# Layer 3 of a four-layer network from sums of the token-major residual, with layer 0's output statistics on ACT and the gate's factor on POOL

## The chip, the cores and the metric

The program runs on one core of a Trainium2 chip. A core has a matrix engine (TensorE; PE in the profile, with its weight loads as PEld), a vector engine (VectorE, DVE), an activation engine (ScalarE, ACT), a general engine (GpSimd, POOL) and a sequencer that mostly issues transfers (SyncE, SP). They run side by side, each through its own queue in order, and wait for one another on semaphores. SBUF and PSUM are the on-chip memories; the products of PE go to PSUM. The metric is the device time of one execution in microseconds; the profile is one further execution with its trace.

## The reference

Input is `x` of 16 images of 64 x 64 tokens with 256 channels, in f32. Each of four layers adds its output on the group-normalised input to that input:

```python
x = x + L0(gn(x), embeddings)   # nearest of 1024 codes by distance, its row is returned
x = x + L1(gn(x), Wf, bf, Wg, bg, Wh, bh)   # sigmoid attention inside each row of 64 tokens
x = x + L2(gn(x), w1, b1, w2, b2, w3, b3)   # a gate per token, from a softmax over 4096 x 4096
x = x + L3(gn(x), w_qkv, w_out, b_out, gamma, beta)   # linear attention, then a layer norm
```

`gn` has 32 groups of 8 channels over all tokens. The part that the change rewrites most is layer 3:

```python
q, k, v = split(x @ w_qkv)            # 4 heads of 32
q = softmax(q, over the 32 of a head) * 32 ** -0.5
k = softmax(k, over all tokens)
context = einsum('bhdn,bhen->bhde', k, v)
out = einsum('bhde,bhdn->bhen', context, q)      # back to tokens
out = out @ w_out + b_out
out = (out - mean) * rsqrt(var + 1e-3) * gamma + beta   # over the channels
```

## The kernel before

An image (a batch in what follows) has 4096 tokens. Work goes in 8 chunks of 512 tokens (`CH` = 4 tiles of 128), channel-major as two tiles of 128 channels (`NK` = 2). Between layers the activations pass through DRAM, one 512 KB tile for each chunk.

Every layer is a Python generator that emits instructions and yields a number now and then. At the end of the kernel each layer of each batch gets a start and a length in units of the code search, and a heap interleaves the generators by these, so that in the middle of the run the search of one batch lies beside layer 1 of the one before, the exponentials of another and layer 3 of a fourth. The yields set how much of one generator goes between two pieces of another. The framework puts what is emitted into the engines' queues by priority and by its own estimate of readiness; on the chip each queue then runs in order.

The pieces that matter here:

- `stage1` is layer 0. For each tile of 128 tokens PE computes products with 1024 codes (L377), ACT makes the row `nn` of squared lengths (L372), DVE adds and takes the maximum (L384) and finds its place (L389), and POOL gathers the code's row and adds it to the token-major input by an indirect DMA (L390). `back` turns a finished chunk back to channel-major by PE transposes (L352), ACT copies it out of PSUM (L355), and DVE takes statistics of it (`chunk_stats`, L249, aggregated at L256 in `gn_finish`).
- `layer1` has its projections at L457 and L468, `rows2` the three rows of layer 2, `stage2` the 4096 x 4096 exponentials: L617 on ACT and L620 on DVE, 1024 of each, 2048 elements wide.
- `gate2` loads the gates spread over the partitions (`gb`, one buffer), ACT forms the factor `u` = 1 + scale * gate (L674), DVE multiplies (L675) and takes statistics.
- `stage3` is layer 3 in two passes over the chunks. In the first, PE forms keys (L737) and, token-major, queries with values (L759, with a bias row at L763); ACT copies them (L764); keys get a running maximum and exponentials (L740 to L749); queries a softmax over each head by DVE and POOL (L778, L779, L780, and `normalize`, L726 to L728); the context is summed (L784, L786). The queries are transposed (L716) and stored. In between, the context becomes `wctx`, and a Gram matrix `gram` for the variance. In the second pass `form` multiplies the Gram matrix with the queries (L826, L828), `variance` sums this over partitions by matrix products with a column of ones (L834), ACT adds epsilon (L836), POOL takes the power -0.5 (L837), both one chunk ahead of use; PE forms the output (L854), ACT scales it (L857), PE transposes the residual (L859) and adds `x_row` (L863), DVE adds both (L865), and SP stores it.

PSUM has a pool `ps_m` of four banks that nearly all stages share through `bank`. `xb`, with three buffers, holds the chunks of the first statistics, of `rows2` and of both passes of layer 3.

Of the kernel before, what the change touches and what calls it, by code (L numbers as in the profile page):

```python
# [21 lines left out]
CH = 4  # L22
# [19 lines left out]
def kernel(  # L42
# [64 lines left out]
    nc.vector.memset(eps3, 1e-3)  # L107
# [17 lines left out]
    def row_tile(name):  # L125
        t = const.tile([P, C], BF16, name=name)
        nc.gpsimd.memset(t, 0.0)
        return t

    h_row, qv_row, x_row = row_tile("h_row"), row_tile("qv_row"), row_tile("x_row")  # L130

    def twice(row):
        return row.unsqueeze(1).to_broadcast([P, 2, C])

    def put_row(dst, v, weight, tag, plus=None):

        v3 = small.tile([P, NK, PARTS], F32, tag="v3", name=f"v3_{tag}")
        nc.scalar.copy(v3, v.unsqueeze(2).to_broadcast([P, NK, PARTS]))
        pb = bank(f"prow_{tag}")
        row = pb[:PARTS, :C]  # L140
        weight(row, v3, plus)

        for n in range(PARTS - 1):
            top = small.tile([PARTS, C], BF16, tag="ptop", name=f"top_{tag}_{n}", bufs=1)
            nc.scalar.copy(top, row)
            nc.tensor.matmul(row, lhsT=below[:, n, :], rhs=top, start=False, stop=True, skip_group_check=True)
        nc.scalar.copy(dst[0:PARTS, :], row)
# [47 lines left out]

    def centred(src, name):
# [22 lines left out]
    one = const.tile([P, 1], F32, name="one")  # L219
    nc.vector.memset(one, 1.0)  # L220
# [30 lines left out]
    def gn_finish(st, kind, b):  # L251

        tag = f"{kind}_{b}"
        mv = small.tile([P, NK, 2], F32, tag="gn_mv", name=f"mv_{tag}")
        for k in range(NK):
            nc.vector.bn_aggr(mv[:, k, :], st[:, k, :, :].rearrange("p c s -> p (c s)"))  # L256
        mean = mv[:, :, 0]
# [45 lines left out]
    def stage1(b):  # L303
        tag = f"s1_{b}"
        scale, _, nbias = norm0.pop(b)
# [39 lines left out]
        st1 = stats_tile(1, f"st1_{tag}")  # L345
        x1_d[b] = []

        def back(ch):
            for k in range(NK):
# [5 lines left out]
                nc.scalar.copy(xt[ch][:, k, :], pt)  # L355
            chunk_stats(st1, xt[ch], ch)
# [52 lines left out]
        with tc.high_priority(offset=URGENT):  # L409
            norm1[b] = gn_finish(st1, "n1", b)  # L410
# [5 lines left out]
    def layer1(b):  # L416
# [34 lines left out]
        def attend(ch):  # L451
# [14 lines left out]
            for t in range(CH):  # L466
# [5 lines left out]
                if t % 2 == 1:  # L472
                    nc.tensor.matmul(
                        ph[:, t - 1 : t + 1, :], lhsT=ones3, rhs=twice(h_row), start=False, stop=True, skip_group_check=True
# [178 lines left out]
    def gate2(b):  # L653
# [9 lines left out]
        for ch in range(NCHUNK):  # L663
# [8 lines left out]
            for k in range(NK):  # L672
                u = s3p.tile([P, CW], F32, tag="u2", name=f"u_{tag}_{ch}_{k}")
                nc.scalar.activation(u, gb, AF.Identity, bias=one, scale=scale[:, k : k + 1])  # L674
# [14 lines left out]
    def stage3(b):  # L689
# [6 lines left out]
        wqv_n = wts.tile([P, NK, 2 * P], F32, tag="wqv_n", name=f"wqv_{tag}")  # L696
        nc.sync.dma_start(out=wqv_n[:, :, 0:P], in_=w_src[:, :, 0, :])
        nc.sync.dma_start(out=wqv_n[:, :, P:], in_=w_src[:, :, 2, :])
        with tc.high_priority(offset=URGENT):
            scaled(wk_n, scale, nc.scalar)  # L700
            scaled(wqv_n, scale, nc.vector)
            put_row(qv_row, nmean, by_weight(wqv_n), f"qv_{tag}")
# [6 lines left out]
        ctxa = wts.tile([P, P], F32, tag="ctxa", name=f"ctx_{tag}")  # L709
        qvs, qTs = {}, []  # L710

        def queries(ch):
            qv = qvs.pop(ch)
            pq = bank(f"pq_{tag}_{ch}")
            for t in range(CH):
                nc.tensor.transpose(pq[:, t * P : (t + 1) * P], qv[:, t, 0, :], ident)  # L716
            qT = s3p.tile([P, CW], F32, tag="v2", name=f"qT_{tag}_{ch}", bufs=4)
            nc.scalar.activation(qT, pq, AF.Copy, scale=float(DH ** -0.5))
            qd_ = dram.tile([P, CW], F32, tag=f"qT_{ch}", name=f"qd_{tag}_{ch}")
            nc.scalar.dma_start(out=qd_, in_=qT)  # L720
            qTs.append(qd_)

        def normalize(ch):
            q4 = qvs[ch][:, :, 0, :].rearrange("p t (h d) -> p t h d", d=DH)
            qd = small.tile([P, CH, HEADS], F32, tag="qd", name=f"qd_{tag}_{ch}")
            nc.vector.tensor_reduce(qd, q4, AX.X, ALU.add)  # L726
            nc.vector.reciprocal(qd, qd)  # L727
            nc.gpsimd.tensor_tensor(q4, q4, qd.unsqueeze(3).to_broadcast([P, CH, HEADS, DH]), ALU.mult)  # L728

        for ch in range(NCHUNK):  # L730
# [14 lines left out]
            kx = s3p.tile([P, CW], F32, tag="v2", name=f"kx_{tag}_{ch}", bufs=4)  # L745
# [6 lines left out]
            qv = s3p.tile([P, CH, 2, P], F32, tag="u4", name=f"qv_{tag}_{ch}")  # L752
            qvs[ch] = qv
            for pr in range(CH // 2):
                pqv = bank(f"pqv_{tag}_{ch}_{pr}").rearrange("p (j n) -> p j n", j=2)
                for j in range(2):
                    t = 2 * pr + j
                    for k in range(NK):
                        nc.tensor.matmul(  # L759
                            pqv[:, j, :], lhsT=xt[:, k, t * P : (t + 1) * P], rhs=wqv_n[:, k, :],  # L760
                            start=(j == 0 and k == 0), stop=False, skip_group_check=True,
                        )
                nc.tensor.matmul(pqv, lhsT=ones3, rhs=twice(qv_row), start=False, stop=True, skip_group_check=True)  # L763
                nc.scalar.copy(qv[:, 2 * pr : 2 * pr + 2, :, :].rearrange("p j s n -> p j (s n)"), pqv)  # L764
            if ch == 0:
                put_row(x_row, xm_, by_identity, f"x_{tag}")
            yield 5
# [3 lines left out]
            ek = s3p.tile([P, CH, P], F32, tag="v2", name=f"ek_{tag}_{ch}", bufs=4)  # L771
            nc.scalar.copy(ek.rearrange("p t d -> p (t d)"), pkt)
            if ch > 0:
                queries(ch - 1)
# [170 lines left out]
```

## Time and profile before

| | |
|---|---|
| runs of the kernel | median 5933.36 us of 3 (5928.48 to 5943.17) |
| profiled execution | 5928.44 us, span 5926.7 us, mean clock of PE 0.941 |
| instructions | 79,561 |
| HBM | 751.18 MB read, 303.04 MB written, 178 GB/s over the span |
| L620 (DVE), L617 (ACT) | 1024 each; mean 2302 ns and 2088 ns |
| L377 (PE) | 4096 passes, mean 623 ns |
| L390 (POOL) | 512 gathers, mean 2067 ns |
| L779, L728 (POOL) | 128 each; mean 1818 ns and 1561 ns |

A busy time is the part of the span in which at least one instruction of the engine ran. For PE it includes the time in which a product drains, so the mean of a matmul is longer than what it keeps from the next one; an f32 matmul shows as two passes. In rows of waits the columns are the time in total, how often, and the longest. Every engine is busy nearly all of the run; the first 800 us or so fill the interleaving (layer 3 first appears at 807 us) and the last 130 us hold layer 3 of the last batch alone.

### The profile page before, as it was taken

The numbers are of one execution on the slowest core, as the hardware profiler recorded it, in microseconds if no ns is written. First come the engines' busy times: TensorE is split into PE (matmuls) and PEld (weight loads), VectorE is DVE, ScalarE is ACT, GpSimd is POOL, SyncE is SP. The second block draws the span as 40 slices with busy tenths as digits, with TensorE's granted clock in tenths as the row PEclk, the third lists the DMA queues.
The fourth block names the chain that finished last, engine by engine and source line by source line (L and its number), as shares of the span: only waits on it lengthen the run. The fifth ranks groups of instructions, "written<-read, shape, count | busy, mean of one in ns | idle before, by whom it ended". The sixth has DMA issues, their size and how long they took to land.

```text
span 5926.7 us, 79561 instructions
## 1 busy us (share of the span) xinstructions
PE 5337.4 (90%) x28239; PEld 3211.1 (54%) x28239; DVE 5121.1 (86%) x7282; ACT 4570.8 (77%) x6754; POOL 1939.4 (33%) x1314
## 2 busy tenths in 40 slices
PE   8968899889999999998989999898999989997777
PEld 3524465545656565564656556565555646564555
DVE  6499798989989898898989889898998989888882
ACT  4377687878778787887879788797878878787873
POOL 3122233224233332433334233342424333231331
PEclk9989999989999898999999899999999999998899
DMA  6544745555656656565665656656565664644543
GB/s 186 162 124 124 225 137 177 184 184 162 207 168 192 197 151 202 184 207 181 184 205 167 194 183 188 206 174 204 164 210 164 202 204 147 209 158 173 184 158 116
DMA packets 521380, 1059.47 MB, mean 179 GB/s; under 512 B 52504, under 2 KB 266392, under 8 KB 512792
## 3 DMA queue, kind: packets, MB, share of 16 engines
q1 hardware_dynamic: 406288, 885.11, 44.7%
q0 software_dynamic: 73728, 67.14, 7.9%
q10 hardware_dynamic: 40968, 102.13, 4.5%
q8 instruction: 224, 3.67, 0.3%
q14 instruction: 172, 1.41, 0.1%
HBM read 751.18 MB, written 303.04 MB: 178 GB/s over the span
## 4 chain that ended last, share of the span: by engine, by line
PE 48%; DVE 16%; ACT 12%; DMA 7%; issue 6%; POOL 4%; ACTq 0%; SPq 0%; POOLq 0%; DVEq 0%
PE pd_s L377 15%; DVE ex_s L620 6%; ACT ex_s L617 5%; PE ph_l L468 5%; PE pqv_s L759 3%; PE po_s L854 3%; PE pk_s L737 3%; PE po_l L506 2%; PE pr_r L565 2%; DMA xr_r<-x_l 2%; DVE i_s L389 2%; POOL qv_s L779 2%; PE pvr_s L834 1%; PE pz_s L826 1%; DMA qo_s<-qd_s 1%
## 5 line engine op out<-in xcount | busy, mean ns | idle before, releaser
L620 DVE CUSTOM_DVE_ANT_0 ex_s<-ex_s,x2b 128x2048 f32<-128x2048 f32 x1024 | 2350.7, 2302 | 46.2 <-ACT ex_s L617 44.9
L617 ACT ACTIVATE ex_s<-x0b,nmax_s,x_r 128x2048 f32<-128x2048 f32 x1024 | 2137.8, 2088 | 66.4 <-DVE num_s L620 60.3
L377 PE MATMUL pd_s<-e,xn_s 128*128 128x512 f32 x4096 | 2022.2, 623 | 43.5 <-DVE m L384 40.8
L390 POOL DMA_INDIRECT xc_s<-in_emb_rows,i_s x512 | 1058.1, 2067 | 2063.9 <-DVE i_s L389 1466.8
L377 PEld LDWEIGHTS pd_s<-e,xn_s 128*128 128x128 f32 x4096 | 754.4, 197 | 764.9 <-issue 669.1
L384 DVE CUSTOM_DVE_ANT_0 nd_s<-pd_s,nn_s 128x1024 f32<-128x1024 f32 x512 | 622.2, 1215 | 174.4 <-ACT nn_s L372 82.1
L389 DVE FIND_INDEX8 i_s<-m,nd_s 128x8 uint32<-128x1024 f32 x512 | 624.1, 1219 | 0.0
L372 ACT ACTIVATE nn_s<-ne,nx_s 128x1024 f32<-128x1024 f32 x512 | 583.2, 1141 | 21.5 <-DVE nx_s L343 15.7
L468 PE MATMUL ph_l<-wh_l,xt_l 128*128 128x256 f32 x2048 | 525.5, 393 | 28.3 <-DVE m L384 16.5
L759 PE MATMUL pqv_s<-wqv_s,xk_s 128*128 128x256 f32 x2048 | 494.6, 382 | 0.0
L759 PEld LDWEIGHTS pqv_s<-wqv_s,xk_s 128*128 128x128 f32 x2048 | 390.9, 192 | 127.5 <-issue 65.5
L468 PEld LDWEIGHTS ph_l<-wh_l,xt_l 128*128 128x128 f32 x2048 | 380.9, 193 | 143.8 <-issue 57.5
L837 POOL TENSOR_TENSOR lrs_s<-lrs_s,mhalf 128x4 f32<-128x4 f32 x128 | 183.0, 1429 | 749.3 <-ACT lrs_s L836 710.5
L857 ACT ACTIVATE y_s<-po_s,lrs_s 128x256 f32<-128x256 f32 x512 | 237.1, 469 | 214.8 <-PE po_s L854 166.2
L854 PE MATMUL po_s<-wctx_s,qo_s 128*128 128x256 f32 x1024 | 336.0, 415 | 32.3 <-ACT y_s L857 31.1
L506 PE MATMUL po_l<-at_l,h_l 64*128 64x64 f32 x4096 | 318.5, 297 | 46.2 <-DVE xt_l L511 42.7
L506 PEld LDWEIGHTS po_l<-at_l,h_l 64*128 64x128 f32 x4096 | 286.5, 206 | 108.5 <-DVE xt_l L511 48.9
L779 POOL TENSOR_TENSOR qv_s<-qv_s,qm_s 128x512 f32<-128x512 f32 x128 | 232.7, 1818 | 312.3 <-DVE qm_s L778 181.7
L728 POOL TENSOR_TENSOR qv_s<-qv_s,qd_s 128x512 f32<-128x512 f32 x128 | 199.8, 1561 | 304.6 <-DVE qd_s L727 252.9
L865 DVE TENSOR_TENSOR y_s<-pxo_s,y_s 128x512 f32<-128x512 f32 x256 | 175.2, 686 | 125.0 <-ACT y_s L857 123.2
L854 PEld LDWEIGHTS po_s<-wctx_s,qo_s 128*128 128x128 f32 x1024 | 178.2, 198 | 172.5 <-ACT y_s L857 84.7
L737 PE MATMUL pk_s<-xk_s,wk_s 128*128 128x512 f32 x512 | 269.6, 650 | 0.0
(195 smaller groups left out, 7519.8 us busy)
## 6 DMA issues: line engine op xcount, KB each, us to landing
xs_s<-in_xT SPq DMA_DIRECT2D x128, 512.0 KB
xt_s<-in_xT SPq DMA_DIRECT2D x128, 512.0 KB
xc_s<-in_x SPq DMA_DIRECT2D x128, 512.0 KB
x_s<-xt_s ACTq DMA_DIRECT2D x128, 512.0 KB
xt_l<-x_s SPq DMA_DIRECT2D x128, 512.0 KB
x_l<-xt_l SPq DMA_DIRECT2D x128, 512.0 KB
xr_r<-x_l SPq DMA_DIRECT2D x128, 512.0 KB
xg_g<-x_l SPq DMA_DIRECT2D x128, 512.0 KB
```

The lines of the kernel that those rows point to most:

```text
L372: nc.scalar.activation(nn, ne2, AF.Identity, bias=nx2[ch][:, t : t + 1])
L377: nc.tensor.matmul(pd[:, cols], lhsT=xn[ch][:, k, t * P : (t + 1) * P], rhs=e2[:, k, cols], start=(k == 0), stop=(k == NK - 1),)
L384: nc.vector.tensor_tensor_reduce(out=nd, in0=pd, in1=nn, scale=1.0, scalar=-3.0e38, op0=ALU.add, op1=ALU.max, accum_out=m8[:, 0:1],)
L389: nc.vector.max_index(i8, m8, nd)
L390: nc.gpsimd.indirect_dma_start(out=xc[ch][:, t, :], out_offset=None, in_=emb_rows, in_offset=bass.IndirectOffsetOnAxis(ap=i8[:, 0:1], axis=0),
L468: nc.tensor.matmul(ph[:, t, :], lhsT=X[:, k, t * P : (t + 1) * P], rhs=wh_n[:, k, :], start=(t % 2 == 0 and k == 0), stop=False, skip_grou ...
L506: nc.tensor.matmul(po[:, r, k * CH + t, :], lhsT=h[rows, t, k * P : (k + 1) * P], rhs=at[rows, t, :], start=True, stop=True,)
L617: nc.scalar.activation(ex, x0b, AF.Exp, bias=nmax[:, T : T + 1], scale=x01[:, T, 1:2], accum_out=den[:, h, T : T + 1])
L620: nc.vector.tensor_tensor_reduce(out=ex, in0=ex, in1=x2b, scale=1.0, scalar=0.0, op0=ALU.mult, op1=ALU.add, accum_out=num[:, h, T : T + 1],)
L737: nc.tensor.matmul(pk, lhsT=wk_n[:, k, :], rhs=xt[:, k, :], start=(k == 0), stop=(k == NK - 1))
L759: nc.tensor.matmul(pqv[:, j, :], lhsT=xt[:, k, t * P : (t + 1) * P], rhs=wqv_n[:, k, :], start=(j == 0 and k == 0), stop=False, skip_group ...
L854: nc.tensor.matmul(po[:, j, :], lhsT=qT[:, t * P : (t + 1) * P], rhs=wctx[:, 1, :], start=True, stop=True)
```

## The change

Four things are done.

1. Layer 3 leaves the values out. It uses that the context is linear in them: instead of keys times values it sums keys times the token-major residual (256 wide, `gather`), and multiplies these sums by the values' weights once per batch. For this the residual's transposes and `x_row` move from the second pass into the first; ACT copies them out of PSUM, and they are stored to DRAM and loaded again, token-major, in the second pass. The query product is 128 wide instead of 256. The transposes of the queries move to the second pass.
2. The variance no longer comes from the Gram matrix: ACT squares the output in PSUM and sums, into a tile `junk` and an accumulator. `gam` is multiplied by 16, the square root of `C`, and `eps3` by `C`, so that the sum needs no division. DVE then multiplies by the factor and `gamma`, and POOL adds the residual.
3. In layer 0's `back` ACT's copy also sums and a second ACT instruction squares in place and sums; DVE's statistics there go, and five small DVE instructions make mean and variance.
4. In `gate2` POOL forms the factor `u`.

The yields in the first pass are 4 and 6 instead of 5 and 5; the buffers `v2` go from four to three.

```diff
-                nc.scalar.copy(xt[ch][:, k, :], pt)
-            chunk_stats(st1, xt[ch], ch)
+                nc.scalar.activation(xt[ch][:, k, :], pt, AF.Copy, accum_out=st1[:, 0, k, ch : ch + 1])
+                nc.scalar.activation(
+                    pt, pt, AF.Square, bias=nshift[:, k : k + 1], accum_out=st1[:, 1, k, ch : ch + 1]
+                )
...
-            norm1[b] = gn_finish(st1, "n1", b)
+            nc.vector.tensor_reduce(sums, st1, AX.X, ALU.add)
+            nc.vector.tensor_scalar(mv[:, :, 0], sums[:, 0, :], 1.0 / TOK, None, ALU.mult)
+            nc.vector.tensor_tensor(off, mv[:, :, 0], nshift, ALU.add)
+            nc.vector.tensor_tensor(off, off, off, ALU.mult)
+            nc.vector.scalar_tensor_tensor(
+                mv[:, :, 1], sums[:, 1, :], 1.0 / TOK, off, op0=ALU.mult, op1=ALU.subtract
+            )
+            norm1[b] = gn_ends(mv, "n1", b)
...
-                nc.scalar.activation(u, gb, AF.Identity, bias=one, scale=scale[:, k : k + 1])
+                nc.gpsimd.tensor_scalar(u, gb, scale[:, k : k + 1], 1.0, ALU.mult, ALU.add)
...
+        def gather(ch):
+            pc = bank(f"pc_{tag}_{ch}")
+            ek, xr = eks.pop(ch), res.pop(ch)
             for t in range(CH):
+                nc.tensor.matmul(pc[:, :C], lhsT=ek[:, t, :], rhs=xr[:, t, :], start=(t == 0), stop=(t == CH - 1))
+            if ch > 0:
+                nc.vector.scalar_tensor_tensor(
+                    sums, sums, al[:, ch : ch + 1], pc[:, :C], op0=ALU.mult, op1=ALU.add
+                )
...
+                        pq[:, t, :], lhsT=xt[:, k, t * P : (t + 1) * P], rhs=wq_n[:, k, :],
...
+            if ch > 0:
+                gather(ch - 1)
+            yield 4
...
+                nc.tensor.matmul(px, lhsT=ones3, rhs=repeated(x_row, 2), start=False, stop=True, skip_group_check=True)
+                nc.scalar.copy(xr[:, 2 * pr : 2 * pr + 2, :], px)
+            d = dram.tile([P, CH, C], F32, tag=f"xr_{ch}", name=f"xd_{tag}_{ch}")
+            nc.scalar.dma_start(out=d, in_=xr)
...
+            nc.scalar.activation(q4s[ch], q4s[ch], AF.Exp)
+            if ch > 0:
+                store_q(ch - 1)
+            yield 6
...
+                    nc.tensor.matmul(
+                        po[:, j, :], lhsT=qT[:, t * P : (t + 1) * P], rhs=wctx, start=True, stop=True
+                    )
+                    nc.scalar.activation(junk, po[:, j, :], AF.Square, accum_out=rs[:, j : j + 1])
+                nc.scalar.activation(rs, rs, AF.Identity, bias=eps3)
+                nc.gpsimd.tensor_tensor(rs, rs, mhalf[:, 0:2], ALU.pow)
+                for j in range(2):
+                    t = 2 * pr + j
+                    nc.vector.scalar_tensor_tensor(
+                        y[:, t, :], po[:, j, :], rs[:, j : j + 1], gam, op0=ALU.mult, op1=ALU.mult
+                    )
...
+                    xrs[ch] = xb.tile([P, CH, C], F32, tag="xb", name=f"xo_{tag}_{ch}")
+                    nc.sync.dma_start(out=xrs[ch], in_=xds[ch])
+                    if ch + 1 < NCHUNK:
+                        queries(ch + 1)
                 yield 3
+            nc.gpsimd.tensor_tensor(y, y, xrs.pop(ch), ALU.add)
```

## The prediction

> **What bounds the kernel now.** The page's first part, then one window over the repeating middle. The code search of a batch (32 FIND_INDEX8 of L389 each) starts at 1723 us for one batch and at 4894 us for the ninth after it: a batch takes 3171/9 = 352 us. Columns: length, then busy time of PE, PEld, DVE, ACT, POOL, then clock, DMA share, GB/s.
>
> ```profile
> PE 5337.4 (90%) x28239; PEld 3211.1 (54%) x28239; DVE 5121.1 (86%) x7282; ACT 4570.8 (77%) x6754; POOL 1939.4 (33%) x1314
> 1723.00:4894.00 3171.00, 2957.86 (x15878) 1793.36 (x15877) 2855.46 (x4060) 2563.17 (x3790) 1123.61 (x729) 0.96 0.61 188
> ```
>
> PE shows 93% there, DVE 90%, ACT 81%, POOL 35%. PE's figure counts drains. What a matmul keeps from the next is seen in the timeline of PE, in the tail, where layer 3 of the last batch runs alone:
>
> ```profile
> 5814.48 1.88 PE L737 MATMUL pk_s<-xk_s,wk_s 128*128 128x512 f32 x4
> 5816.20 1.89 PE L759 MATMUL pqv_s<-wqv_s,xk_s 128*128 128x256 f32 x8
> 5817.93 0.38 PE L763 MATMUL pqv_s<-qv_row,ones 128*128 128x512 bf16 x1
> 5818.14 1.89 PE L759 MATMUL pqv_s<-wqv_s,xk_s 128*128 128x256 f32 x8
> 5819.87 0.38 PE L763 MATMUL pqv_s<-qv_row,ones 128*128 128x512 bf16 x1
> 5820.09 0.60 PE L770 MATMUL pkt_s<-ident,kx_s 128*128 128x128 f32 x4
> 5820.52 0.60 PE L716 MATMUL pq_s<-ident,qv_s 128*128 128x128 f32 x4
> 5821.41 1.16 PE L784 MATMUL pc_s<-qv_s,ek_s 128*128 128x128 f32 x8 [0.29 <-ACT ek_s L772]
> ```
>
> Start to start, a pass of 512 f32 columns costs (5816.20-5814.48)/4 = 0.43 us, of 256 columns 1.73/8 = 0.216, of 128 columns 0.11, of one column (L834, same view) also 0.11, the bf16 row 0.21. With these and the counts of every group I get some 4,560 us of PE slots, 77% of the span: PE has room. DVE at 90% in the middle is the nearest to a bound, and its waits are short ones behind the others:
>
> ```profile
> DVE y_s L865 <- ACT y_s L857: 123.2, 81, 4.3
> ...
> DVE nd_s L384 <- ACT nn_s L372: 82.1, 59, 7.3
> ...
> DVE qz_s L828 <- PE pz_s L826: 52.7, 33, 5.9
> ...
> DVE xg_g L675 <- ACT u_g L674: 25.0, 16, 7.4
> ...
> DVE st_s L249 <- ACT xt_s L355: 18.8, 23, 3.8
> ```
>
> All but the second belong to instructions that the change removes or rewires: 220 us. The chain of waits says the same: it is long rows of L617, L620 and L377, no single stall.
>
> One more thing limits DVE, seen in the timelines of DVE and POOL:
>
> ```profile
> 3457.04 2.94 DVE L620 CUSTOM_DVE_ANT_0 ex_s<-ex_s,x2b 128x2048 f32<-128x2048 f32 x1
> 3456.79 1.04 POOL L779 TENSOR_TENSOR qv_s<-qv_s,qm_s 128x512 f32<-128x512 f32 x1 [7.15 <-DVE nkm_s L740]
> ```
>
> L620 takes 2.28 us; begun under a POOL operation it took 2.94. The other way, POOL's 128x512 takes 1.05 us alone and up to 3.1 behind an L620.
>
> **What the Trainium skill says.** GPSIMD Engine Reference, Specifications: the SBUF interfaces are shared with VectorE, with contention for DVE instructions in a 2-port mode or with two SBUF inputs. The trace agrees: L620 and L675 (two SBUF inputs) stretch, L384 and L511 (one in PSUM) do not. TensorE: Matmul & The Clock Gate, Step-by-step: back-to-back the gap is the streamed columns; agrees down to 128 columns, and at one column the trace has a floor of 0.11. Prices: ScalarE: Activation LUTs, What ACT_TABLE_LOAD costs: about 93 ns per pointer operand; GPSIMD Engine Reference, Elementwise: 769 ns for a 512-element one-input loop.
>
> **PE.** 128 chunks in all. Queries alone instead of queries and values: 2048 passes from 256 to 128 columns, 2048 x (0.216-0.11) = -217. Bias rows 256 to 128: -27. pz gone: 256 x 0.43 = -110. pvr gone: 1024 x 0.11 = -113. The context product becomes 256 columns wide: 1024 x (0.216-0.11) = +109. Transposes are moved, not saved. Sum -358 us, 8% of the slots. Since PE isn't the bound this pays only through waits.
>
> **DVE.** Out, from the groups by shape: L249 on xt_s 163.9, its 32 aggregates 10.8, L828 87.3, L865 175.2, context 42.9, wctx 14.1: 494. In: 512 scalar_tensor_tensor of 128x256 from PSUM at the 0.482 of L805 = 247; sums 112 x 0.482 + 16 x 0.42 = 61; wctx 16 x 0.42 = 7; the five small operations that finish layer 0's statistics 16 x 1.0 = 16: 331. Net -163. Against it stands the shared interface. Now 256 POOL operations of 1.05 us stretch L620 by 22 us (58 of 1024 visibly) and L675 by 15, 0.14 each. New are 256 factors of about 0.8 us and 128 residual additions of 1024 elements, 2.1 us (twice 1.05): by length 0.11 and 0.28 each, +28 and +35. Bounds: nothing, and 256 x 0.8 + 128 x 2.1 = 474 if each blocks fully. I take 63. DVE: -100, to 5,020.
>
> **ACT.** Out: L355 139.4, u 199.3, qv copies 146.1, y 237.1, lrs 33.3, wT and gram 10.2: 765. In: 256 copies with a sum, 0.601 (L718) + 0.194 (L746's accumulator read) = 203; 256 squares with bias and sum, 0.674 + 0.194 (L746) = 222; 128 query copies 75; 256 residual copies at 0.578 = 148; 512 squares of 256 elements with sum, L857's 0.469 less a pointer's 0.093 plus 0.19 = 290; 256 small at 0.26 = 67; two kinds per batch 17: 1,022. Net +257, and 128 more DMA issues at 0.33 on ACT's queue (42, not in busy time). ACT: 4,828 busy, about 5,000 with all its issues (131 now): level with DVE. Its sums alone would still allow 352 us a batch.
>
> **POOL.** Factors 256 x (0.8+0.6), additions 128 x (2.1+0.6), pow 128 x 1.43 to 256 x 1.0, where 0.6 is the mean wait on DVE that L779 and L728 show (1.82 and 1.56 against 1.05). +775, to 2,715, 46%. No bound, but in order: behind each addition or factor wait gathers (L390), pow and the next factor.
>
> **What the new work stands in front of.** In layer 0 two squares of 0.87 us join each chunk's two copies on ACT: behind them wait the nn of the next token tiles, and DVE's L384 behind those (82 us today), and the store of x1; nn has five buffers, so it can be made ahead. Uncovered this is 128 x 1.7 = 218 us, the case of B. In layer 3 the 1.2 us of residual copies per chunk stand ahead of the query exponentials, which nobody needs before the next chunk. On SP the output's store waits for POOL's addition instead of DVE's (115 us at L867 now), with the next chunk's loads behind it.
>
> **DMA and queues.** The token-major residual is stored once more: 128 x 512 KB, 67 MB on 1,059, share 0.61 to about 0.65. xk is held longer (until its transposes after the next yield), and SP, which already waits 310 us for it at L732, waits longer; prefetch of depth three covers it, as PE shows no wait on xk at all. If not, PE's wait on xk is 128 short ones of up to 1 us, in the upper end of the range. The first transfer of the factor waits on POOL instead of ACT (433 us of SP waits at L667 today).
>
> **Sum.** DVE's -100 are 6.3 us a batch; at 90% use 7.0 us of the period. From layer 3's start (807) to the last batch's (5440) there are 4633/352 = 13.2 periods: -92. Earlier, DVE isn't the bound: nothing. Tail: the first half of layer 3 stays at PE's pace (7.93 us a chunk; 1.72+1.79+0.22+0.44+0.87+0.43+1.73 = 7.2 slots against 7.38): -1. The second half runs 6.7 us a chunk (pz at 5894.78, 5901.49, 5908.15) waiting in turn on y and qo; after, POOL (2 x 0.75 + 2.1) or the 1.3 MB a chunk at the 333 GB/s that 120 GB/s at share 0.36 implies give about 4 to 5: some -14 with the last addition in it. New waits of DVE on POOL I set equal to the 220 us that go. 5928 - 92 - 15 = 5,821 for the profiled execution; the median of the runs stands 5 us above it: 5,826.
>
> **Rivals.**
> A, PE's relief counts: pz's wait and L865's vanish unreplaced, DVE's use in the middle rises from 90 to 93.5%: 314/0.935 = 336 us a batch, -16 x 13.2 - 20: about 5,700. For it: 358 us of slots and three PSUM banks fewer per chunk. Against: po's banks are held through square, pow and two DVE operations.
> B, ACT eats it: level with DVE, it makes nn and ex late; DVE waits on ACT, 378 us now, grow by 100: 5,930.
> C, slower. DVE now waits on POOL at 512 places: 256 pairs (pow before the two products, with no chunk of lead; before, it was computed a chunk ahead) and 256 factors. POOL is in order and waits itself for L620. At 0.43 us each they replace what went; at (107+220)/512 = 0.64 the gain is gone; at 0.8 it is 410-220-107 = +83: about 6,010. For it: even with a chunk's lead ACT waited 40 us on pow, and POOL's operations stretch to 3 us. Against: the pair's wait can be filled by L620.
>
> **Numbers.** Forecast 0.38 (own range 5,770 to 5,880), A 0.27, B 0.10, C 0.25. Faster and slower start at 0.3%, what this measurement can tell. Faster 0.65, same 0.09, slower 0.26. Range 5,660 to 6,020, from A past C.
>
> **What would show it.** DVE busy near 5,020, ACT 4,830, POOL 2,700, PE down; L620's mean up from 2,302 ns by 20 to 50; batch period 345. Wrong if POOL's row heads DVE's waits with over 330 us, if ACT's idle falls to nothing, or if the period falls below 340.

## The result, and the profile after

The changed kernel takes 6270.2 us (median of 4 runs, 6259.62 to 6274.51) against 5936.44 us (4 runs, 5928.48 to 5943.17) of the kernel before: a ratio of 1.056, 95% interval 1.0541 to 1.0579. It is 334 us slower, where the prediction had it 107 us faster, and lies outside the range. The profiled execution took 6271.01 us (span 6269.3 us, mean clock of PE 0.884 instead of 0.941).

First the changed kernel's page, busy time of each engine:

```profile
PE 5242.1 (84%) x26815; PEld 3088.9 (49%) x26815; DVE 5111.9 (82%) x7186; ACT 4670.8 (75%) x8050; POOL 2754.5 (44%) x1842
```

Only POOL is busy for over 100 us more, and each of PE, DVE and ACT has a smaller share of a longer span. The time is idle time. Then the window over nine batches of the repeating middle of the changed kernel; columns as in the prediction:

```profile
1794.00:5200.00 3406.00, 2934.07 (x15073) 1738.46 (x15073) 2863.56 (x4005) 2618.56 (x4517) 1584.10 (x1026) 0.89 0.59 186
```

A batch now takes 3406/9 = 378.4 us instead of 352.3. 26 us times 13 periods are some 340 us, about the whole loss; the tail, where layer 3 of the last batch is alone, went from 133 to 123 us. In these nine batches DVE is busy for 2864 us, before 2855: the same work, and 227 us more of standing still. PE's clock is 0.89 instead of 0.96.

What DVE waited for in the changed kernel (total, how often, longest, in us):

```profile
DVE y_s L891 <- POOL lrs_s L888: 276.3, 169, 4.3
...
DVE ex_s L638 <- ACT ex_s L635: 102.3, 73, 7.1
DVE nd_s L392 <- PE pd_s L385: 79.9, 41, 13.5
DVE nkm_s L773 <- PE pk_s L770: 70.2, 48, 5.1
DVE xg_g L693 <- POOL u_g L692: 67.2, 39, 3.3
DVE qd_s L742 <- ACT q_s L826: 67.1, 43, 2.6
```

The list is headed by POOL's power, and POOL's factor (L692) stands in it as well, 343 us together. The others are spread: many waits between the engines are somewhat longer, though not all (DVE's on ACT's nn fell from 82 to 60 us). PE and ACT have such rows too. First PE, then ACT, in the changed kernel:

```profile
PE px_s L336 <- ACT sq_s L330: 89.3, 42, 6.5
PE pd_s L385 <- DVE m L392: 89.1, 52, 4.0
```

```profile
ACT xrow_s L341 <- PE px_s L336: 185.0, 75, 6.4
...
ACT al_s L777 <- DVE nkm_s L776: 121.4, 40, 9.6
```

Before, the same four were 63.7, 40.8, 69.2 and 24.1 us. The changed kernel's page gives the clock that PE was granted in 40 slices of the span, in tenths (9 is 0.9 or more); the first fence is the changed kernel, the second the kernel before:

```profile
PEclk9989898889899898989989899898988989997778
```

```profile
PEclk9989999989999898999999899999999999998899
```

The records behind it know only two values, 1.0 and 0.5. They add up to 702 us of half clock before and 1462 us after.

Where in a batch the time is lost is seen when each batch is cut by layer 3's own products in the trace: the first pass from the first key product to the first output product, the second from there to the last output product, and the gap to the next batch's first pass. Means of eight batches in the middle; "exponentials" are the DVE instructions of L620/L638 begun in it, 64 a batch whatever the kernel, so the time for one is a measure of pace.

| | first pass: us, PE busy, half clock us, exponentials | us each | second pass: us, exponentials | us each | gap: us, exponentials | us each |
|---|---|---|---|---|---|---|
| before | 174.9, 97%, 3.6, 32.0 | 5.5 | 115.2, 18.9 | 6.1 | 61.4, 13.1 | 4.7 |
| after | 203.3, 88%, 30.6, 33.0 | 6.2 | 103.0, 17.0 | 6.1 | 72.1, 14.0 | 5.1 |

The first pass, into which the change moves the residual, lost its pace; the second pass kept it, though its half-clock time rose from 8.5 to 22.8 us. The gap, which has no product of layer 3's tokens, also got slower: its half-clock time rose from 16.7 to 25.7 us.

A stretch of the timeline of the changed kernel, inside a first pass (start, us, engine, instruction, and idle time before it with what ended it):

```profile
3283.68 0.63 PE L336 MATMUL px_s<-sq_s,neg 128*32 128x128 f32 x2 [5.23 <-ACT sq_s L330]
...
3284.24 2.07 PE L385 MATMUL pd_s<-e,xn_s 128*128 128x512 f32 x2
...
3287.23 1.98 PE L385 MATMUL pd_s<-e,xn_s 128*128 128x512 f32 x4
...
3287.44 1.66 POOL L803 TENSOR_TENSOR q_s<-q_s,qm_s 128x512 f32<-128x512 f32 x1
...
3287.70 4.21 DVE L638 CUSTOM_DVE_ANT_0 ex_s<-ex_s,x2b 128x2048 f32<-128x2048 f32 x1
...
3288.67 1.09 POOL L692 TENSOR_SCALAR u_g<-gb_g,s_n 128x512 f32<-128x512 f32 x1
```

PE stands for 5.23 us. Where it starts again the clock records show 0.5 for 3.41 us, and two passes of the code search take 2.07 us; the next four, at full clock, take 1.98. An L638, 2.28 us when alone, takes 4.21 with two POOL operations begun just before and under it.

### The profile page after: what moved, and what is told of

The parts are those of the page before. It is cut to its first block, busy times and chain, and to the rows that moved or that the text cites. A ratio compares the mean times of both kernels' runs of the same rounds, so it can differ in the third digit from the quotient of the medians.

```text
span 6269.3 us, 78925 instructions
## 1 busy us (share of the span) xinstructions
PE 5242.1 (84%) x26815; PEld 3088.9 (49%) x26815; DVE 5111.9 (82%) x7186; ACT 4670.8 (75%) x8050; POOL 2754.5 (44%) x1842
## 2 busy tenths in 40 slices
DMA packets 539820, 1126.55 MB, mean 180 GB/s; under 512 B 54552, under 2 KB 268440, under 8 KB 531224
## 4 chain that ended last, share of the span: by engine, by line
PE 32%; DVE 17%; POOL 10%; issue 9%; ACT 8%; DMA 7%; ACTq 0%; POOLq 0%; SPq 0%; DVEq 0%
PE pd_s L385 11%; DVE ex_s L638 6%; PE ph_l L486 3%; ACT ex_s L635 3%; POOL xc_s L398 2%; POOL lrs_s L888 2%; PE pk_s L770 2%; PE pr_r L583 2%; DMA xr_r<-x_l 2%; DVE nd_s L392 2%; DMA xs_s<-in_xT 2%; PE pc_s L750 2%; DVE i_s L397 2%; DVE y_s L891 2%; PE pq_s L789 2%
## 5 line engine op out<-in xcount | busy, mean ns | idle before, releaser
L638 DVE CUSTOM_DVE_ANT_0 ex_s<-ex_s,x2b 128x2048 f32<-128x2048 f32 x1024 | 2455.5, 2407 | 102.8 <-ACT ex_s L635 102.3
L385 PE MATMUL pd_s<-e,xn_s 128*128 128x512 f32 x4096 | 2101.9, 645 | 136.4 <-DVE m L392 89.1
L398 POOL DMA_INDIRECT xc_s<-in_emb_rows,i_s x512 | 1165.0, 2275 | 1729.4 <-DVE i_s L397 1160.3
L385 PEld LDWEIGHTS pd_s<-e,xn_s 128*128 128x128 f32 x4096 | 783.7, 204 | 911.9 <-issue 691.5
L883 PE MATMUL po_s<-wctx_s,qT_s 128*128 128x256 f32 x1024 | 383.0, 481 | 124.5 <-DVE y_s L891 53.4
L888 POOL TENSOR_TENSOR lrs_s<-lrs_s,mhalf 128x2 f32<-128x2 f32 x256 | 303.9, 1194 | 383.3 <-ACT lrs_s L887 363.5
L692 POOL TENSOR_SCALAR u_g<-gb_g,s_n 128x512 f32<-128x512 f32 x256 | 325.7, 1281 | 287.8 <-DMA gb_g<-gd_s 155.5
L891 DVE SCALAR_TENSOR_TENSOR y_s<-po_s,lrs_s,gam 128x256 f32<-128x256 f32 x512 | 225.1, 477 | 277.3 <-POOL lrs_s L888 276.3
L902 POOL TENSOR_TENSOR y_s<-y_s,xo_s 128x1024 f32<-128x1024 f32 x128 | 363.4, 2839 | 172.0 <-DVE y_s L891 158.7
L886 ACT ACTIVATE junk<-po_s 128x256 f32<-128x256 f32 x512 | 194.0, 379 | 218.5 <-PE po_s L883 170.7
L883 PEld LDWEIGHTS po_s<-wctx_s,qT_s 128*128 128x128 f32 x1024 | 206.1, 230 | 286.1 <-ACT junk L886 93.1
L789 PEld LDWEIGHTS pq_s<-wqv_s,xk_s 128*128 128x128 f32 x2048 | 256.7, 196 | 84.9 <-issue 59.5
L693 DVE SCALAR_TENSOR_TENSOR xg_g<-xg_g,nm_n,u_g 128x512 f32<-128x512 f32 x256 | 227.9, 904 | 74.6 <-POOL u_g L692 67.2
```

Of the source, the lines that this page charges most:

```text
L385: nc.tensor.matmul(pd[:, cols], lhsT=xn[ch][:, k, t * P : (t + 1) * P], rhs=e2[:, k, cols], start=(k == 0), stop=(k == NK - 1),)
L398: nc.gpsimd.indirect_dma_start(out=xc[ch][:, t, :], out_offset=None, in_=emb_rows, in_offset=bass.IndirectOffsetOnAxis(ap=i8[:, 0:1], axis=0),
L638: nc.vector.tensor_tensor_reduce(out=ex, in0=ex, in1=x2b, scale=1.0, scalar=0.0, op0=ALU.mult, op1=ALU.add, accum_out=num[:, h, T : T + 1],)
L883: nc.tensor.matmul(po[:, j, :], lhsT=qT[:, t * P : (t + 1) * P], rhs=wctx, start=True, stop=True)
L888: nc.gpsimd.tensor_tensor(rs, rs, mhalf[:, 0:2], ALU.pow)
```

## The experiments

Three explanations were open: POOL in front of DVE (rival C) with the shared SBUF interface behind it; PE short of work and therefore at half clock; and layer 3's passes, with more now in the first one, in a bad proportion to the rest. All ratios are to the kernel before, run on the same chip, with their 95% interval; what a version of the changed kernel gives back is counted from 6270.2 us.

### One part undone in the changed kernel

A pair of lead for the power: the two products on DVE are issued one pair of token tiles later, and POOL's addition and the store of the output move along with them.

```diff
-                for j in range(2):
-                    t = 2 * pr + j
-                    nc.vector.scalar_tensor_tensor(
-                        y[:, t, :], po[:, j, :], rs[:, j : j + 1], gam, op0=ALU.mult, op1=ALU.mult
-                    )
+                if pending is not None:
+                    finish(*pending)
+                pending = (ch, pr, po, rs)
```

> The changed kernel with the two products of a pair issued one pair later, so that POOL's power has a pair of lead; nothing is left out, two PSUM banks are held instead of one. T1 (DVE stands behind POOL's power and factor, in order and without lead): DVE's wait on POOL at y falls from 276 us to under 100 and the time from 6,270 to 6,100 to 6,150. T2 (POOL's SBUF operations shut DVE out of the shared interface): the mean of ex_s on DVE stays at 2.41 us, and the time within 30 us. T3 (ACT's new squares in layer 0 delay the search): no change. T4 (SP's queue stands at the output's store, which waits for POOL's addition): no gain, as the store comes later still.

Measured: 6168.23 us, 1.039 (1.0352 to 1.0428), 102 us back. In DVE's waits of this kernel:

```profile
DVE y_s L880 <- POOL lrs_s L899: 178.5, 131, 4.3
```

The wait fell by 98 us, and the time by about as much. So in this kernel DVE's waits on the power count, as far as the later addition and store have no part in it.

The factor on ACT again, and the residual's addition on DVE instead of POOL:

```diff
-                nc.gpsimd.tensor_scalar(u, gb, scale[:, k : k + 1], 1.0, ALU.mult, ALU.add)
+                nc.scalar.activation(u, gb, AF.Identity, bias=one, scale=scale[:, k : k + 1])
```

```diff
-            nc.gpsimd.tensor_tensor(y, y, xrs.pop(ch), ALU.add)
+            nc.vector.tensor_tensor(y, y, xrs.pop(ch), ALU.add)
```

> The changed kernel with the gate's factor on ACT again, as before the change. T1: the 67 us of DVE's wait on u go and POOL's queue is 326 us shorter, so that the wait on the power falls too, to about 200: 6,120 to 6,170. T2: mean of ex_s from 2.41 to about 2.36 us, 50 us of DVE: 6,200 to 6,230. T3: ACT has 200 us more: 6,300. T4: 6,270.

> The changed kernel with the residual's addition on DVE instead of POOL (128 of 1024 elements, about 1.2 us each, 155 us more DVE). T1: the wait on the power falls to 180 us, DVE's work eats it: 6,270 to 6,320. T2: mean of ex_s to about 2.33 us, 80 us back, against 155: 6,330. T3: 6,330 or more. T4: SP's wait at the output's store falls from 506 us to 150, the loads come earlier, DVE's wait on xs from 57 to under 20: 6,200.

Measured: 6249.47 us, 1.0528 (1.0491 to 1.0566), and 6205.07 us, 1.0455 (1.0418 to 1.0492). The factor is worth 21 us, the addition 65. With the addition on DVE the mean of L638 falls from 2407 to 2325 ns: 1024 x 82 ns = 84 us of DVE's time were the price of POOL's 128 additions. T4 had named the time, 6,200, but not for the right reason: SP's wait at the store fell to 413 us and not to 150, and DVE's wait on xs stayed at 57. L638 in the changed kernel, by the groups of DVE (busy us, mean ns, idle before):

```profile
L638 DVE CUSTOM_DVE_ANT_0 ex_s<-ex_s,x2b 128x2048 f32<-128x2048 f32 x1024 | 2455.5, 2407 | 102.8 <-ACT ex_s L635 102.3
```

Layer 0's output statistics on DVE again:

```diff
-                nc.scalar.activation(xt[ch][:, k, :], pt, AF.Copy, accum_out=st1[:, 0, k, ch : ch + 1])
-                nc.scalar.activation(
-                    pt, pt, AF.Square, bias=nshift[:, k : k + 1], accum_out=st1[:, 1, k, ch : ch + 1]
-                )
+                nc.scalar.copy(xt[ch][:, k, :], pt)
+            chunk_stats(st1, xt[ch], ch)
...
-            norm1[b] = gn_ends(mv, "n1", b)
+            norm1[b] = gn_finish(st1, "n1", b)
```

> The changed kernel with layer 0's output statistics on DVE again (bn_stats), ACT only copying. DVE has about 165 us more, ACT 270 us less. T1, T2 and T4: DVE is what the waits add to, so 6,350 to 6,420. T3: 6,050 to 6,150, with ACT's waits and DVE's wait on nn down.

Measured: 6155.9 us, 1.0372 (1.0335 to 1.0409). DVE's busy time rises by 111 us to 5223 and the program gets 114 us faster. More work on the engine taken for the bound, and less time: the first sign that DVE's sum isn't what sets the period (ACT has less to do here as well).

The power left out, ACT's sum used as it is:

```diff
-                nc.gpsimd.tensor_tensor(rs, rs, mhalf[:, 0:2], ALU.pow)
```

> The changed kernel without POOL's power: DVE multiplies by the sum plus epsilon as it comes from ACT, so the output is not scaled by the inverse deviation; 256 POOL operations of about 1.2 us are left out and one engine less stands between the squares and the products. T1: DVE's wait at y falls from 276 us to under 100 (on ACT instead) and the time to 6,080 or less, about as much as the lead gave or more. T2: the power reads two elements and hardly holds the interface: 6,250.

Measured: 6087.53 us, 1.0263 (1.023 to 1.0295), 183 us back, with this left of the wait:

```profile
DVE y_s L890 <- ACT lrs_s L887: 47.8, 48, 5.7
```

Even with no power at all nearly half of the loss stays, and the first pass of a batch takes 203.7 us as before (with the lead 203.3): what the power costs lies in the second pass and the gap.

All four together (lead, factor on ACT, addition and statistics on DVE), which leaves the sums and the squares:

> The changed kernel with all four edits of the first runs together: the products one pair later, the factor on ACT, the addition on DVE, layer 0's statistics on DVE. What is left of the change is the sums over the residual and the variance by squares. Alone the four gave 102, 20, 65 and 115 us (6,270 less each median). If each cost is its own, they add to 302: 5,970. If they draw on the same slack (DVE's idle time), the second helps less than the first: 6,040 to 6,090. If the core of the change were the main cost: above 6,090.

Measured: 6131.19 us, 1.0354 (1.0323 to 1.0385). One by one the four gave 102 + 21 + 65 + 114 = 302 us, together 139. L638 is back at 2303 ns, so the shared interface is paid off, and DVE waits on the power for only 52.8 us; 3.5% remain. The first pass takes 192.2 us, hardly less than with the statistics alone on DVE (190.8).

### One part alone in the kernel before

The statistics on ACT alone (the edit of the change), and the factor on POOL alone:

```diff
-                nc.scalar.copy(xt[ch][:, k, :], pt)
-            chunk_stats(st1, xt[ch], ch)
+                nc.scalar.activation(xt[ch][:, k, :], pt, AF.Copy, accum_out=st1[:, 0, k, ch : ch + 1])
+                nc.scalar.activation(
+                    pt, pt, AF.Square, bias=nshift[:, k : k + 1], accum_out=st1[:, 1, k, ch : ch + 1]
+                )
```

```diff
-                nc.scalar.activation(u, gb, AF.Identity, bias=one, scale=scale[:, k : k + 1])
+                nc.gpsimd.tensor_scalar(u, gb, scale[:, k : k + 1], 1.0, ALU.mult, ALU.add)
```

> The kernel before with layer 0's output statistics on ACT alone. Theory of the prediction (DVE's busy time sets the period): 165 us of DVE go, 5,830. Theory T3 (ACT's squares stand in front of what the search needs, and cost about what undoing them gave): 6,030 to 6,050. T5 (they cost only because ACT has the rest of the change to carry too): 5,900 to 5,950.

> The kernel before with the gate's factor on POOL alone. T1 (POOL's queue in front of DVE): DVE's wait on u rises from 25 to 65 us and POOL is late for the gathers: 5,950 to 6,000. T2 (shared interface alone, 256 x 0.1 us): 5,950. Theory of the prediction (ACT relieved by 200 us, DVE slowed by 28): 5,930 to 5,950.

Measured: 5994.28 us, 1.0123 (1.009 to 1.0156), and 5975.92 us, 1.0094 (1.0059 to 1.0128). The first takes 115 us from DVE (5121 to 5006) and makes the program 66 us slower.

The disputed rule by itself: nothing is added, and DVE is given less to do. Layer 0's output statistics are taken of the first chunk of each batch only.

```diff
-            chunk_stats(st1, xt[ch], ch)
+            if ch == 0:
+                chunk_stats(st1, xt[ch], ch)
...
-            norm1[b] = gn_finish(st1, "n1", b)
+            norm1[b] = gn_finish(st1[:, :, 0:1, :], "n1", b)
```

> The kernel before with layer 0's output statistics from the first chunk alone: 224 bn_stats of 0.68 us (152 us of DVE) are left out and nothing takes their place. The prediction's rule (DVE's busy time over 90% sets the period): 13.2/16 of 152/0.9 = 139 us less, 5,790. T7's reading (chains of waits through several engines set it, and DVE only takes part): 5,850 to 5,920.

Measured: 5950.45 us, 1.0033 (1.0019 to 1.0047). Its page:

```profile
PE 5317.9 (89%) x28239; PEld 3193.9 (54%) x28239; DVE 5018.4 (84%) x7058; ACT 4565.1 (77%) x6754; POOL 1958.4 (33%) x1314
```

DVE's busy time falls by 103 us to the very 5,020 of the prediction, the other engines have nothing more to do, and the time does not fall.

The variance by squares alone, on the values' context (no Gram matrix, no product with ones, the power without lead):

```diff
-            pz = bank(f"pz_{tag}_{ch}")
-            nc.tensor.matmul(pz, lhsT=gram, rhs=qs[ch], start=True, stop=True)
...
-                    nc.scalar.activation(y[:, t, :], po[:, j, :], AF.Copy, scale=rs[:, t : t + 1])
+                    nc.scalar.activation(y[:, t, :], po[:, j, :], AF.Square, accum_out=rs[:, j : j + 1])
...
+                nc.scalar.activation(rs, rs, AF.Identity, bias=eps3)
+                nc.gpsimd.tensor_tensor(rs, rs, mhalf[:, 0:2], ALU.pow)
+                for j in range(2):
+                    t = 2 * pr + j
+                    nc.vector.scalar_tensor_tensor(
+                        y[:, t, :], po[:, j, :], rs[:, j : j + 1], gam, op0=ALU.mult, op1=ALU.mult
+                    )
```

> The kernel before with the variance by squares alone: no Gram product, no product with ones (223 us of PE slots go), the power right between squares and products, DVE scales and then adds the residual from PSUM (247 us more DVE, 87 less). T1 (POOL's power without lead): DVE's wait at y on POOL of 150 us or more, 6,080 or more. T6: half-clock time well over 702 us, and the time over 6,050. The prediction's rule: 160 us more DVE, 6,070. If the sums are the costly half of the core instead: under 6,000.

Measured: 5946.7 us, 1.0039 (1.0024 to 1.0055). DVE is busy for 117 us more than in the kernel before (5238), PE's half-clock time is 882 us instead of 702, and the time rises by 0.4%.

These squares, the statistics on ACT and the factor on POOL, all three edits above in the kernel before: everything of the change but the sums and what goes with them (the residual in the first pass, its store and load, POOL's addition).

> The kernel before with three of the four parts: variance by squares, layer 0's statistics on ACT, factor on POOL, but values and context as before and the residual transposed in the second pass. Alone they gave +23, +66 and +48 us. T10 (the sums over the residual, with what they move into the first pass, are the main cost): 6,030 to 6,080, so that the sums stand for 190 us or more of the 334. If the parts aggravate each other instead (all engines near their limit): above 6,150.

Measured: 5927.11 us, 0.9997 (0.9985 to 1.0009). Its page, and DVE's first wait in it:

```profile
PE 5153.3 (87%) x26863; PEld 3050.9 (52%) x26863; DVE 5145.6 (87%) x7443; ACT 4588.8 (77%) x7874; POOL 2341.8 (40%) x1698
```

```profile
DVE y_s L858 <- POOL lrs_s L855: 130.9, 105, 6.7
```

This is the run that decides, and it came out below all that was expected of it: where 190 of the 334 us or more were put down to the sums, the whole loss is gone without them. Here too DVE waits on a power without lead, ACT takes the squares of two layers and POOL forms the factor; over half of PE's relief is there (pz and pvr, 223 of the 358 us of slots); and nothing is lost. The first pass takes 179.6 us with 10.7 us of half clock, the second 109.6. Set beside each other: the sums on top of the squares cost 1.0354/1.0039 = 1.031 (the two differ in the lead of the power and a few buffers as well); statistics, factor, addition and lead cost 1.056/1.0354 = 1.020 where the sums are there, while statistics and factor are worth 0.9997/1.0039 = 0.996 where they are not. The parts are not additive, and the sums decide what the others cost.

### The clock

Products that change nothing: one to three bf16 products per token tile ahead of L385 (L377 in the kernel before), each 512 columns wide, which the real product then overwrites.

```diff
+                warm = ones3.unsqueeze(1).to_broadcast([P, 4, P])
+                for _ in range(3):
+                    nc.tensor.matmul(pd[:, 0:512], lhsT=ones3, rhs=warm, start=True, stop=True, skip_group_check=True)
```

> The changed kernel with three bf16 products of 512 columns put in front of each token tile's distances, into the same bank, which the real product then overwrites: 1,536 passes of 0.216 us, 330 us more PE work, about what the change took away. T6 (the change leaves PE idle so often that its clock is halved for 1,462 us of the run instead of 702, and PE's work in those stretches, at half speed, is what makes the period longer): half-clock time falls to 900 us or less and the time to 6,100 or less, in spite of the added work. T7 (half clock is only the sign of idle time, whose cause lies with DVE, ACT and POOL): the time stays at 6,270 or rises by up to 330.

> The kernel before with the same three fillers. T6: there is less half-clock time to win (702 us), and PE has 330 us more: 5,900 to 6,050. T7: 5,980 to 6,200, as PE then has 4,890 us of slots.

> The changed kernel with one filler instead of three (110 us of PE work). T6: a third of the effect of three, 6,200 to 6,230. T7: 6,270 to 6,350.

Measured: three in the changed kernel 6190.3 us, 1.0439 (1.041 to 1.0468); three in the kernel before 6061.34 us, 1.0206 (1.017 to 1.0242); one in the changed kernel 6300.78 us, 1.0617 (1.0585 to 1.0649). The window of the changed kernel with three:

```profile
1794.00:5200.00 3406.00, 3068.89 (x16430) 1817.42 (x16430) 2938.41 (x4127) 2677.59 (x4633) 1584.13 (x1062) 0.94 0.61 191
```

The same useless work, 512 x 3 x 0.215 = 330 us of PE slots, costs the kernel before 122 us and gives the changed kernel 80 back. Half-clock time falls from 1462 to 1008 us there, and in a window of the same 3406 us DVE and ACT are busy for 75 and 59 us more than without it. With equal filler the change costs 6190.3 - 6061.3 = 129 us instead of 334. This would fit a halved clock that makes waiting longer, and doesn't show it: one product per tile left half-clock time at 1357 us and gained nothing, and three change the order of the products too, which alone can give as much (next part). Nor does half-clock time by itself mean loss: the squares alone have 882 us of it and the kernel without the sums 892, with 0.4% and nothing lost. The share of the clock in the loss is not settled.

### The order

Layer 3 begins a little later in the interleaving, in either kernel:

```diff
-LAG4 = 0.04
+LAG4 = 0.05
```

> The kernel before with layer 3 started 0.05 instead of 0.04 units after the gate (LAG4): not an instruction more or less, only the order in the queues. T8 (the order before is a fitted one, and any edit that reshuffles it costs on the order of a per cent, whatever it removes): 5,960 to 6,020. Without T8: within 20 us of 5,930.

> The changed kernel with the same LAG4 of 0.05. T8: the changed kernel's order is one draw of many, so it moves by 30 to 100 us, down as easily as up. Without T8: within 20 us of 6,270.

Measured: 5924.22 us, 1.0001 (0.9982 to 1.002), before; 6193.21 us, 1.0457 (1.0422 to 1.0492), after. Yields as before the change, and then more of the period for the first pass and less for the second:

```diff
-            yield 4
+            yield 5
...
-            yield 6
+            yield 5
```

> The changed kernel with yields of 5 and 5 in layer 3's first pass, as before the change, instead of 4 and 6. T8: moves by up to 100 us either way. Without T8: within 20 us of 6,270.

```diff
-            yield 4
+            yield 6
...
-            yield 6
+            yield 8
...
-                yield 3
+                yield 1.5
```

> The changed kernel with yields of 6 and 8 in layer 3's first pass and 1.5 in the second (before: 4, 6 and 3), which spreads the heavier first pass over more of the period. T10 with the place (the first pass grew from 175 to 203 us a batch, with PE at half clock for 31 us of it instead of 4, while the second pass got short of PE work): 6,120 to 6,200. T7 (waits on POOL and ACT wherever they stand): 6,240 to 6,310.

Measured: 6279.51 us, 1.0604 (1.0567 to 1.064), and 6181.9 us, 1.0417 (1.0396 to 1.0439). A mere shift costs the kernel before nothing and gives the changed one 77 us; more room for the first pass gives 88. In the latter the first pass holds 47 exponentials in 252.4 us, 5.4 us each, the pace of the kernel before; but the second pass then has 12 in 80.8 us, 6.7 each. The slow stretch moved. So some 80 of the 334 us hang on the order alone, and the yields of 4 and 6 are not the cause; whether an order fitted anew to the sums would give more was not tried. No version tried beats the kernel before; the one without the sums equals it.

## Why the prediction was wrong

**The step that failed first is the rule of the sum: "DVE's -100 are 6.3 us a batch; at 90% use 7.0 us of the period."** It reads a busy share of 90% as a bound. In the kernel with the statistics of one chunk, DVE's busy time fell by 103 us with nothing added elsewhere, and the time rose by 0.3%; with the statistics on ACT it fell by 115, and the time rose by 1.2%; in the changed kernel 111 us more on DVE went with 114 us less. A busy share says that an engine is seldom idle, not that the period ends when its work ends. Here PE, DVE and ACT at 93, 90 and 81% hand work to each other in fixed orders; that these hand-overs set the period is what fits the runs, not something that one of them shows. The -92 us had no ground.

**The place of the work moved into the first pass was put at nothing, and here lies the loss: "In layer 3 the 1.2 us of residual copies per chunk stand ahead of the query exponentials, which nobody needs before the next chunk."** For the middle of the run the moved work got no price but its rows in the sums of PE, DVE and ACT; that the first half of layer 3 "stays at PE's pace" was worked out for the tail alone. The first pass took 203.3 us instead of 174.9, and PE's busy share in it fell from 97 to 88%. With the four other parts undone it takes 192.2 us at 90%; without the sums 170.9 (squares alone) to 183.5 (statistics alone on ACT) at 94 to 97%, the kernel with added products apart. That the loss stands with the sums is shown.

Two of DVE's waits tell the kernels with the sums from those without: for the query exponentials (`qd_s`), and for the chunks of the first statistics (`xs`). First the changed kernel, then the kernel before, then the one with all but the sums:

```profile
DVE qd_s L742 <- ACT q_s L826: 67.1, 43, 2.6
...
DVE st_s L251 <- DMA xs_s<-in_xT: 57.4, 29, 4.5
```

```profile
DVE qd_s L726 <- ACT qv_s L780: 20.4, 25, 1.8
...
DVE st_s L249 <- DMA xs_s<-in_xT: 13.3, 12, 5.1
```

```profile
DVE qd_s L742 <- ACT qv_s L796: 33.1, 26, 3.7
...
DVE st_s L250 <- DMA xs_s<-in_xT: 12.2, 6, 4.3
```

So the next chunk came to wait for the exponentials. "Prefetch of depth three covers it" did hold for xk, on which PE has no wait in the changed kernel either; but `xs` takes its buffers from the same pool `xb`, and DVE came to wait for it. That the longer hold of xk is the reason is likely, not shown. Together the two grew by 91 us. With more room for the first pass (yields of 6 and 8) they are back at 35.8 and 14.9 us, and 88 us of the loss with them, but other waits grew there. Which piece makes the rest is open: the residual's copies on ACT, the longer hold of xk, the store and reload, or the wider context product. The fourth buffer of `v2` is hardly missed: ACT is idle ahead of kx for 9.1 us, before 9.0. None of the pieces was taken out alone; of what goes with the sums only the addition on POOL was (65 us).

**"PE isn't the bound, this pays only through waits"** held, as 223 us of slots fewer changed nothing in the kernel without the sums, and had a second half that the prediction missed. The Trainium skill says (TensorE: Matmul & The Clock Gate, Part 1: The HAM clock gate) that PE's clock passes all pulses or half of them, by how busy PE was in windows of 3.413 us. The traces agree: only 1.0 and 0.5 occur, and of the 181 low stretches after the change 53 last 3.4 us, 76 last 6.8 and 27 last 10.2. Work taken from PE leaves emptier windows, and those ahead of a drop slow the work that follows: half-clock time is 702 us before, 882 with 223 us of slots fewer (squares alone) and 1462 after. The code search, 4096 passes in both kernels, first after and then before (busy us, mean ns, idle before):

```profile
L385 PE MATMUL pd_s<-e,xn_s 128*128 128x512 f32 x4096 | 2101.9, 645 | 136.4 <-DVE m L392 89.1 <-DVE xt_l L529 36.9 <-ACT h_l L495 5.0
```

```profile
L377 PE MATMUL pd_s<-e,xn_s 128*128 128x512 f32 x4096 | 2022.2, 623 | 43.5 <-DVE m L384 40.8 <-ACT xn_s L322 2.3 <-DVE xt_l L511 0.2
```

80 us more for the same products. PE's busy time fell by 95 us only, where 358 us of slots were taken out. What starts PE's shortage, and how much of the loss the clock adds, stays open.

**The shared interface, "I take 63"**, was mis-sized: L638 costs 105 ns more, 107 us, and L693 904 instead of 800 ns, 27 us; 134 in all, inside the bounds given (0 to 474). The addition, priced at 35, cost 84. These 71 us over the estimate are most of why DVE's busy time fell by 9 us and not by 100.

**ACT, +257**: measured +100. The groups came out as priced (residual copies 141 for 148, squares in layer 3 with their reads 296 for 290), and the durations of all of ACT's instructions add up to 258 us more; but a busy time counts overlapping instructions once, and of the 431 us of accumulator reads 380 lie over other instructions. The sum of rows isn't the busy time. Rival B did not come: DVE's waits on ACT, which were to grow by 100 us, fell from 378 to 301. ACT's share of 75% doesn't clear it all the same: with the statistics taken off it 114 us came back.

**"New waits of DVE on POOL I set equal to the 220 us that go"**: 343 us came. The row of the power itself stands at 276, short of the 330 named as proof, and the factor adds 67. Over 512 places this is 0.67 us each, just past the 0.64 from which rival C decides, so C named the right side and place. Its own sum would then be 343 - 327 = 16 us, not 334, and the kernel with all but the sums has C's power without lead at no loss. C is a part of the loss in the changed kernel (102 us by the lead, 183 without the power), but not its root.

**Right**: POOL 2,715 forecast, 2,754.5 measured; HBM's 67 MB more (1,126.55 moved), though DMA's share in the middle fell to 0.59 over the longer period, where 0.65 was forecast. **The tail** is right by luck: 10 us less measured for 15 forecast, but 7 of them in its first pass, which was to give 1, and 2 to 3 in the rest, which was to give 14.

## What to carry to other kernels

Before a change is priced by the busiest engine, take work from that engine in a throwaway version and see whether the time moves; at 90% busy it may not move at all. Where engines hand work to each other in fixed orders, moving a stage's work from one pass to another is a change of its own, to be judged by cutting the trace at the passes, and parts that cost one per cent alone may cost nothing or two together. When a buffer is held longer, look at every user of its pool. Where PE isn't the bound, count its half-clock time beside its slots, since relief can slow it, but don't take that time for loss.

## What the hardware showed that was not expected

- PE's clock has two values, and a kernel in which PE is busy 84 to 90% of the span spends 12 to 23% of it at the lower one (702 of 5927 us, 1462 of 6269 us). In the 3.4 us ahead of a drop PE was busy 40% on average before and 32% after.
- Work without a use can shorten a program: 330 us of filler on PE made the changed kernel 80 us faster, and the kernel before 122 us slower. A shift of the order without a use for it made the changed one 77 us faster.
- An L638 can take nearly twice its time (4.21 instead of 2.28 us) when POOL operations fall on it. Of 1024, 34 took over 2.4 us before and 105 after; with the 128 additions moved to DVE, 51.
- POOL's own operations suffer too. The groups of POOL in the changed kernel (busy us, mean ns, idle before) show the addition at 2.84 us and the factor at 1.28 us on average; half of the factors take 0.69 us or less, where the prediction priced 0.8, and half of the additions 2.37 us or less.

```profile
L902 POOL TENSOR_TENSOR y_s<-y_s,xo_s 128x1024 f32<-128x1024 f32 x128 | 363.4, 2839 | 172.0 <-DVE y_s L891 158.7 <-issue 4.6 <-DVE gate_s L646 3.3
L692 POOL TENSOR_SCALAR u_g<-gb_g,s_n 128x512 f32<-128x512 f32 x256 | 325.7, 1281 | 287.8 <-DMA gb_g<-gd_s 155.5 <-DVE xg_g L693 110.8 <-DVE nkm_s L776 5.6
```
